# Order of high and low runs, and where the last projection is summed, in a four-layer conditional-residual kernel

## The chip, the cores and the metric

The kernel runs on one core of a Trainium2 chip. The metric is the device time of one execution in microseconds (us). The profile is that of one execution on the chip; its own time is given beside its span. Engines are named as in the profile: PE is TensorE (PEld its weight loads), DVE is VectorE, ACT is ScalarE, POOL is GpSimd, SP is SyncE, which issues most DMAs.

## The reference

Eight batches of 256 tokens with 1024 features go through four residual layers, each x = x + layer(x):

```python
# L0: dense layer plus a gated mixture of 8 rank-16 experts
base = einsum('btd,od->bto', x, W)
logits = einsum('btd,ed->bte', x, Wr); logits[..., language] += 5
gates = softmax over the two largest logits, zero elsewhere
out = base + 2 * einsum('bter,bte,eor->bto', einsum('btd,erd->bter', x, A), gates, B)
# L1: dense layer with bias, plus a per-batch matrix of signs
out = einsum('bsi,oi->bso', x, W) + b + coeff * einsum('bsi,bio->bso', x, 2 * mask - 1)
# L2: a dense layer chosen per batch by its adapter
out = einsum('bsi,boi->bso', x, weight[adapter])
# L3: a rank-16 projection chosen by the same adapter
out = einsum('bnr,bor->bno', einsum('bni,bri->bnr', x, B[adapter]), A[adapter])
```

All inputs and outputs are 32-bit floats (masks and indices are integers).

## The kernel before

**Precision in two parts.** A 32-bit operand is split into a rounded high part (type `fp32r`) and the rest, the low part. A product is high x high + high x low + low x high. `highs(n)` makes the high part of weight block n as a cast on ScalarE (tile `whi`, five buffers), `lows(n)` makes the low part as a subtraction on VectorE (tile `wlo`, four buffers).

**Stages.** Batches are taken in two groups g of four, a group in two pairs q. L0 of a group works on both pairs at once: eight products of quarter matrices (a seven-multiplication scheme with its sums), 16 slots s, with the router, the gates and the experts in between. Then each pair q passes through L1 and L2 in 16 units each. A unit is one output block m (128 of 1024 features) of one batch j of the pair: units run over m, and within m over j. The L3 work of pair q is done beside later units, by short pieces of TensorE work.

**A unit.** `two` (L526 to L542) issues eight matmuls with the high weights against 512 columns, the high and low parts of the activations side by side (L531): the high run. Then come eight matmuls with the low weights against 256 columns, the activations' high part (L540): the low run. Both sum into `po`, one half of a tile `[128, 2, 512]` of 32-bit floats in PSUM, of which there are two. The two batches of one m share a tile (a joint pair), apart from m = 7 of L1 and the last six units of all, which have one each. `early` and `mid` are lists of short pieces that run after the second high matmul and after the high run. The last unit of all uses `three` (L544): its high run takes 16 matmuls with 256 columns (L548), then the low run (L551).

**The order of the work** is written by hand. Each engine executes its instructions in the order of the program, so the slots and units are also a schedule. `unit_slot` issues for unit n, in this order: the load of a later unit (SP), stores, `evacuate` (results of the pair before leave PSUM through ScalarE and VectorE; the sum becomes the next layer's activations, split into high and low parts in the tile `hl` after L1), `highs(n + 4)`, the merging of L1's weights and masks on VectorE, `lows` of three units ahead (`LAGS` delays this near the end of L1), `fold` (a diagonal added on GpSimd), `side` (loads and preparation of L3's weights, splitting of the next pair's activations, `la_parts`, the router) and `main`, the matmuls.

**The head.** `head` issues L0's first two slots in smaller pieces. After it, `l0_slot` calls `highs(5)` and `la_parts(0, 4, 8)`, which casts half of the experts' first factor on ScalarE and subtracts on VectorE (`laghi`, `laglo`), and later `lows`. The work lists of `l0_works` are issued per slot: an entry at s before the slot's matmuls, at -s ahead of its casts. `split_gates(p0)` casts the gated expert sums (`ghi`) on ScalarE and subtracts on VectorE (`glo`); slot 5's matmuls use them. `less` in slot 4 scales two tiles by -1 on ScalarE, then GpSimd issues an accumulating DMA into each.

**The tail.** L3 of the last batch (b = 7) begins with the projection `proj`: block k of the activations against block k of the adapter's factor, with 32 columns of weights; four blocks go to four groups of 32 rows of one bank and run side by side. Blocks 0 to 3 are issued in unit 9 of the last 16. Blocks 4 to 7 are issued after the last unit (L1056), since block 7 comes out of it. A copy to SBUF (L498) and a matmul with a selection matrix (L499) sum the four groups, three times over for three row groups; `third` (L511) makes high and low parts of the result; eight matmuls (L1071) multiply by the other factor. Two blocks leave through ScalarE, after a matmul with the identity has added the old activations in PSUM (L1063); six leave through VectorE in four adds. Their stores are on the queues of SP and ScalarE. Four pieces of the batch before (`fillers`) are also left near the end: two in unit 14, two after the last unit (L1057).

Of the kernel before, what the change touches and what calls it, by code (L numbers as in the profile page):

```python
# [8 lines left out]
F32 = mybir.dt.float32  # L9
# [25 lines left out]
def kernel(ctx: ExitStack, tc: tile.TileContext, x, lang, coeff, ids,  # L35
# [449 lines left out]
    def proj(b, h, n):  # L485
        if h == 0:
            pbs[b] = bank(n, f"pb{b}")
        for g in range(4):
            mm(pbs[b][32 * g:32 * g + 32, :T], l3b[b][:, 4 * h + g, :],  # L489
               xts[b][:, 4 * h + g, :], start=(h == 0), stop=(h == 1))  # L490
        if h == 1:
            pb = pbs.pop(b)
            pr = bank(n + 2, f"pr{b}")
            prs[b] = pr
            if b == NB - 1:

                raw = gp.tile([P, T], F32, tag="lg", name="pbraw", bufs=3)
                copy(raw, pb[:, :T])  # L498
                sums[b] = lambda: mm(pr[:96, :T], sel3_raw, raw, start=True, stop=True)  # L499
                return  # L500
            hi = gp.tile([P, T], FR, tag="lg", name=f"pbhi{b}", bufs=3)
            lo = gp.tile([P, T], FR, tag="lg", name=f"pblo{b}", bufs=3)
            copy(hi, pb[:, :T])
            tt(lo, pb[:, :T], f32(hi), ALU.subtract)

            def both():
                mm(pr[:96, :T], sel3, hi, start=True, stop=False)
                mm(pr[:96, :T], sel3, lo, start=False, stop=True)
            sums[b] = both

    def third(b):  # L511
# [4 lines left out]
        tt(rt[32:64, :], pr[32:64, :T], f32(rt[32:64, :]), ALU.subtract)  # L516
        return rt

    def rank(b):
        sums.pop(b)()  # L520
        rt = third(b)
        for m in range(0, K, 2):
            fillers.append(lambda m=m: finish(b, m, rt, (0, 2)[m // 2 % 2]))


    def two(po, hi, lo, xhl, j, early=(), mid=(), late=()):  # L526


        for k in range(K):
            c = slice(k * P, (k + 1) * P)  # L530
            mm(po, hi[:, c], xhl[:, k, j].rearrange("p h t -> p (h t)"), start=(k == 0),  # L531
               stop=False)
            if k == 1:
                for f in early:
                    f()
        for f in mid:
            f()
        for k in range(K):
            c = slice(k * P, (k + 1) * P)
            mm(po[:, :T], lo[:, c], xhl[:, k, j, 0, :], start=False, stop=(k == K - 1))  # L540
        for f in late:
            f()  # L542

    def three(po, hi, lo, xhl, j):  # L544
        for k in range(K):
            c = slice(k * P, (k + 1) * P)
            for h in range(2):
                mm(po, hi[:, c], xhl[:, k, j, h, :], start=(k + h == 0), stop=False)  # L548
        for k in range(K):
            c = slice(k * P, (k + 1) * P)  # L550
            mm(po, lo[:, c], xhl[:, k, j, 0, :], start=False, stop=(k == K - 1))  # L551
# [117 lines left out]
    def l0_works(g):  # L669


        p0, p1 = pair_of(g, 0), pair_of(g, 1)
        w = {}

        def at(s, *fs):
            w.setdefault(s, []).extend(fs)

        def add(name, h, src):
            nc.gpsimd.dma_start(quad(g, name)[h], src, accum_op=ALU.add)

        def s1_add(h):
            fold_quad(quad(g, "S1")[h], h)
            add("S1", h, w0[1, 2 + h])

        def s3_add(h):
            t = quad(g, "S3")[h]
            copy(flat(t), flat(quad(g, "S2")[h]))
            fold_quad(t, h)
            add("S3", h, w0[1, 2 + h])

        def s4_add(h):
            copy(flat(quad(g, "S4")[h]), flat(quad(g, "S2")[h]))
            add("S4", h, w0[0, 2 + h])

        def less(h, name, j, i):

            t = flat(quad(g, name)[h])
            nc.scalar.mul(t, t, -1.0)  # L698
# [12 lines left out]
        if g == 0:  # L711
            at(1, constants, *both(s1_add))
            at(2, *both(less, "T1", 1, 0), lambda: router([p0]))
            at(3, lambda: weigh([p0]), lambda: expand(p0), lb_parts, *subs("S2", "A11", "S1"))
            at(4, *both(s4_add), lambda: gate(p0))
            at(5, lambda: router([p1]))
            at(6, lambda: weigh([p1]), lambda: expand(p1))
        else:
            at(0, *both(s1_add), *both(less, "T1", 1, 0))
            at(2, lambda: expand(p0))  # L720
            at(3, *subs("S2", "A11", "S1"))
            at(4, *both(s4_add), lambda: gate(p0))
# [12 lines left out]
        return w  # L735
# [59 lines left out]
    def l0_slot(n):  # L795
# [67 lines left out]

    pos_tile = {}

    def main(n):

        kind, q, m, j = slots[n]
# [6 lines left out]
        end = q == 3 and kind == "L2"  # L875
        joint = u < 10 if end else (m < K - 1 or kind == "L2")
# [54 lines left out]
    def side(n):  # L931
# [34 lines left out]
    def unit_slot(n):  # L966
# [18 lines left out]
        evacuate(bulk.pop(0) if not urgent else None)  # L985
        highs(f + HI_AHEAD)
        for work in bulk:
            work()
# [76 lines left out]
    leave = [bank(n, f"po{b}_{n}") for n in (0, 2, 1)]  # L1065

    def place(m):
        return ends[:, m % 2, :T] if m in by_act else leave[m // 2][:, m % 2 * T:m % 2 * T + T]

    for m in (0, *by_act, 1, 2, 3, 4, 5):  # L1070
        mm(place(m), at[:, m * P:(m + 1) * P], rt, start=(m not in by_act), stop=True)  # L1071

    for m0, m1, queue in ((0, 1, nc.sync), (1, 2, nc.sync), (2, 4, nc.sync), (4, 6, nc.scalar)):
        if m0 == 4:
            for i, m in enumerate(by_act):
                copy(xt[:, m, :], ends[:, i, :T])
            nc.scalar.dma_start(out[b, :, K - 2:K, :], xt[:, K - 2:K, :])
        xs = xt[:, m0:m1, :].rearrange("p m t -> p (m t)")
        tt(xs, leave[m0 // 2][:, m0 % 2 * T:m0 % 2 * T + T * (m1 - m0)], xs, ALU.add)
        queue.dma_start(out[b, :, m0:m1, :], xt[:, m0:m1, :])  # L1080


# [55 lines left out]
```

## Time and profile before

| | us |
|---|---|
| median of 3 runs | 605.03 |
| lowest, highest | 604.06, 605.21 |
| the profiled execution | 603.36 |
| its span | 601.0 |
| PE busy in the span | 593.1 |
| DVE busy | 474.2 |
| ACT busy | 385.7 |
| POOL busy | 135.2 |

The span runs from the first to the last instruction on the core; 2.3 us of the execution lie around it. The starts of matmuls are recorded and their ends are modelled, and matmuls overlap with the next one's weight load, so the distance from start to start says how long a matmul holds TensorE, not the duration in a row. A row of a group of instructions has the line of the program, the engine, the operation, output and inputs by the program's names, and a count. In a bracket at its end stands the idle time of the engine ahead of it, and what ended that. Many VectorE operations carry line 68, that of a helper, and are told apart by their tiles.

### The profile page before, as it was taken

What the parts mean: (1) busy time and instruction counts of PE and PEld (TensorE: products, weight loads), DVE (VectorE), ACT (ScalarE), POOL (GpSimd) and SP (SyncE); (2) the same over time, 40 slices, a digit from 0 to 9 for tenths busy, and PEclk for the clock granted to TensorE, in tenths of its full rate; (3) what the DMA queues carried; (4) which work ended last, traced back from release to release, by engine and by line L of the source; (5) the groups of instructions that cost most, each with busy time, mean ns of one, the idle gap of its engine ahead of it and who ended that gap; (6) DMA issues with size and microseconds to landing.
All of it is one profiled execution on the core that took longest, in us unless ns stands there. A gap on an engine that the chain in (4) does not pass through costs nothing.

```text
span 601.0 us, 8936 instructions
## 1 busy us (share of the span) xinstructions
PE 593.1 (99%) x3240; PEld 499.1 (83%) x3240; DVE 474.2 (79%) x561; ACT 385.7 (64%) x457; POOL 135.2 (23%) x174
## 2 busy tenths in 40 slices
PE   9999999999999999999999999999999999999995
PEld 7777888888888888888778888888888888888884
DVE  5579688899699899586755796789978999977853
ACT  5667566687669787543553874568866788864431
POOL 0322250114241213122110234111423111521000
PEclk9999999999999999999999999999999999999998
DMA  8987894667685877599940799836767686847504
GB/s 283 343 199 165 191 233 137 200 235 267 208 278 188 283 257 265 209 347 322 268 70 24 156 249 233 250 105 210 285 204 255 205 294 228 301 154 232 190 1 140
DMA packets 39533, 130.22 MB, mean 217 GB/s; under 512 B 4802, under 2 KB 6466, under 8 KB 38722
## 3 DMA queue, kind: packets, MB, share of 16 engines
q1 hardware_dynamic: 34594, 112.36, 53.7%
q0 software_dynamic: 4608, 16.78, 15.3%
q8 instruction: 25, 0.41, 0.3%
q10 hardware_dynamic: 288, 0.52, 0.3%
q14 instruction: 18, 0.15, 0.1%
HBM read 121.25 MB, written 8.39 MB: 216 GB/s over the span
## 4 chain that ended last, share of the span: by engine, by line
PE 97%; ACT 1%; DVE 1%; issue 0%; DVEq 0%; POOL 0%; POOLq 0%; ACTq 0%
PE po L531 39%; PE mm L599 30%; PE po L540 20%; PE pl L308 1%; PE pf L470 1%; PE pb L442 1%; PE ph L626 1%; PE ph L627 1%; PE ph L625 1%; PE warm L1010 1%; PE pb L489 0%; ACT x L698 0%; DVE c L68 0%; PE po L548 0%; PE pg L392 0%
## 5 line engine op out<-in xcount | busy, mean ns | idle before, releaser
L531 PE MATMUL po<-hl,whi 128*128 128x512 f32 x1016 | 254.5, 392 | 0.0
L531 PEld LDWEIGHTS po<-hl,whi 128*128 128x128 f32 x1016 | 182.8, 189 | 32.7
L68 DVE TENSOR_TENSOR wlo<-raw,whi 128x1024 fp32r<-128x1024 f32 x128 | 160.8, 1266 | 1.3 <-issue 1.2
L540 PEld LDWEIGHTS po<-hl,wlo 128*128 128x128 f32 x1016 | 137.6, 190 | 11.3 <-issue 1.6
L288 ACT CAST whi<-raw 128x1024 fp32r<-128x1024 f32 x128 | 133.7, 1048 | 18.0 <-PE mm L599 8.4
L540 PE MATMUL po<-hl,wlo 128*128 128x256 f32 x1016 | 142.4, 283 | 0.0
L599 PE MATMUL mm<-whi,whi 128*128 128x512 f32 x224 | 88.6, 396 | 0.0
L599 PE MATMUL mm<-wlo,whi 128*128 128x512 f32 x224 | 87.9, 392 | 0.0
L235 POOL TENSOR_TENSOR raw<-raw,ident 128x128 f32<-128x128 f32 x72 | 60.5, 843 | 115.6 <-DMA raw<-in_w 100.8
L257 ACT ACTIVATE raw<-raw,negc,c 128x1024 f32<-128x1024 int32 x64 | 79.5, 1242 | 3.9 <-DMA raw<-in_mask 3.9
L599 PE MATMUL mm<-whi,wlo 128*128 128x512 f32 x224 | 70.8, 391 | 0.0
L68 DVE TENSOR_TENSOR raw<-raw,w 128x1024 f32<-128x1024 f32 x56 | 68.8, 1228 | 1.4 <-issue 1.4
L235 POOL TENSOR_TENSOR w<-w,ident 128x128 f32<-128x128 f32 x28 | 31.1, 1112 | 167.7 <-DMA w<-in_w 120.1
L68 DVE TENSOR_TENSOR wlo<-x,whi 128x1024 fp32r<-128x1024 f32 (+1 forms) x38 | 44.8, 1187 | 11.6 <-issue 6.8
L599 PEld LDWEIGHTS mm<-whi,whi 128*128 128x128 f32 x224 | 42.2, 189 | 11.1 <-issue 1.1
L288 ACT CAST whi<-A 128x1024 fp32r<-128x1024 f32 x26 | 27.3, 1051 | 36.2 <-PE mm L599 24.5
L599 PEld LDWEIGHTS mm<-whi,wlo 128*128 128x128 f32 x224 | 42.2, 188 | 9.2 <-DVE wlo L68 0.2
L599 PEld LDWEIGHTS mm<-wlo,whi 128*128 128x128 f32 x224 | 42.2, 188 | 8.6
L572 ACT COPY c<-po 128x512 f32<-128x512 f32 (+1 forms) x34 | 18.7, 551 | 45.9 <-PE po L540 45.9
L575 ACT ACTIVATE sum<-po,b_sb 128x512 f32<-128x512 f32 (+1 forms) x36 | 23.1, 640 | 31.0 <-PE po L540 30.9
L288 ACT CAST whi<-x 128x1024 fp32r<-128x1024 f32 x34 | 35.2, 1048 | 11.1 <-PE mm L599 8.8
L68 DVE TENSOR_TENSOR c<-mm,c 128x1024 f32<-128x1024 f32 x20 | 24.4, 1221 | 21.8 <-PE mm L599 21.8
(126 smaller groups left out, 523.8 us busy)
## 6 DMA issues: line engine op xcount, KB each, us to landing
raw<-in_mask SPq DMA_DIRECT2D x64, 512.0 KB, 5.4
raw<-in_w SPq DMA_DIRECT2D x64, 512.0 KB, 4.8
w<-in_w SPq DMA_DIRECT2D x28, 512.0 KB, 3.4
out<-c SPq DMA_DIRECT2D x29, 256.0 KB, 3.2
A<-in_w SPq DMA_DIRECT2D x14, 512.0 KB, 8.6
x<-in_x SPq DMA_DIRECT2D x6, 1024.0 KB, 7.8
A<-in_w POOLq DMA_DIRECT2D x12, 512.0 KB, 8.5
x<-in_x POOLq DMA_DIRECT2D x12, 512.0 KB, 8.5
```

Source lines behind the costliest of these rows:

```text
L68: nc.vector.tensor_tensor(o, a, b, op)
L235: (eng or nc.gpsimd).tensor_tensor(t, t, ident, ALU.add)
L257: nc.scalar.activation(f32(raws[n]), raws[n], AF.Identity, bias=negc[:, b:b + 1], scale=c2[:, b:b + 1])
L288: copy(prep_hi(i), flat(source(i)))
L308: mm(pl[c:c + 32, :], wrs[:, k, :], X[g][:, j, k, :], start=(k < 4), stop=(k >= 4))
L442: mm(pb[c:c + 32, j * T:(j + 1) * T], l3b[b][:, k, :], xts[b][:, k, :], start=(k < 4), stop=(k >= 4))
L470: mm(po[:, i * T:(i + 1) * T], at[:, (m + i) * P:(m + i + 1) * P], rt, start=True, stop=True)
L531: mm(po, hi[:, c], xhl[:, k, j].rearrange("p h t -> p (h t)"), start=(k == 0), stop=False)
L540: mm(po[:, :T], lo[:, c], xhl[:, k, j, 0, :], start=False, stop=(k == K - 1))
L572: copy(xs, po[:, :, T:])
L575: nc.scalar.activation(xs, po[:, :, T:], AF.Identity, bias=b1c)
L599: mm(*args, skip_group_check=True, **kw)
```

## The change

`two` becomes `high_run` and `low_run`. The low run of a unit is put into a list, and the list is emptied at the end of a unit that closes its tile: a joint pair is issued as high run of the first batch, high run of the second, low run of the first, low run of the second. In the second unit of a joint pair `lows` is issued after `main`. In L0 of the first group, `lows(5)` is issued right after `highs(5)`, and `split_gates(p0)` moves from the start of slot 5 into slot 4, ahead of `less`. The second `la_parts` moves by two units, from 12 and 13 to 14 and 15.

At the end, blocks 4 to 6 of the last projection and one filler are issued between the high and the low run of the last unit, and their copy to SBUF follows. After the last unit the sum of the seven blocks (L499's matmul) no longer closes its group; one filler follows; then block 7 is multiplied with `b3_last`, its factor laid out three times side by side (96 columns), into the same group. `last_block` makes `b3_last` earlier on VectorE. The results of blocks 0 and 1 get places in PSUM of their own, and the order of the eight matmuls and of the leaving blocks changes.

```diff
@@ def proj(b, h, n)
-        for g in range(4):
-            mm(pbs[b][32 * g:32 * g + 32, :T], l3b[b][:, 4 * h + g, :],
-               xts[b][:, 4 * h + g, :], start=(h == 0), stop=(h == 1))
+        last = b == NB - 1
+        for k in range(4 * h, 4 * h + 4):
+            if last and k == K - 1:
+                continue
+            g = k % 4
+            mm(pbs[b][32 * g:32 * g + 32, :T], l3b[b][:, k, :], xts[b][:, k, :],
+               start=(h == 0), stop=(h == 1 or last and k == 3))
...
-                sums[b] = lambda: mm(pr[:96, :T], sel3_raw, raw, start=True, stop=True)
+                sums[b] = lambda: mm(pr[:96, :T], sel3_raw, raw, start=True, stop=False)
...
+    b3_last = wrs[:, :3, :]
+
+    def last_block():
+        nc.vector.tensor_copy(b3_last, l3b[NB - 1][:, K - 1:, :].to_broadcast([P, 3, 32]))
...
-    def two(po, hi, lo, xhl, j, early=(), mid=(), late=()):
+    def high_run(po, hi, xhl, j, early=(), mid=()):
...
+    def low_run(po, lo, xhl, j, late=()):
...
-    def three(po, hi, lo, xhl, j):
+    def three(po, hi, lo, xhl, j, mid):
...
+        for f in mid:
+            f()
@@ def l0_works(g)
-        at(-5, lambda: split_gates(p0, gts[p0]))
+        at(-5 if g else 4, lambda: split_gates(p0, gts[p0]))
@@ def l0_slot(n)
         if (g, s) == (0, 1):
             highs(5)
+            lows(5)
             la_parts(0, 4, 8)
@@ def main(n)
-            three(po, hi, lo, xh, j)
+            three(po, hi, lo, xh, j, mid=[lambda: proj(NB - 1, 1, 1), fill])
         else:
-            two(po, hi, lo, xh, j, early=early, mid=mid, late=late)
+            high_run(po, hi, xh, j, early=early, mid=mid)
+            low_runs.append(lambda: low_run(po, lo, xh, j, late=late))
         if joint and u % 2 == 0:
             return
+        while low_runs:
+            low_runs.pop(0)()
@@ def side(n)
+        if q == 3 and u == p[1] + 1:
+            last_block()
...
-            if u in (12, 13):
-                la_parts(1, 4 * (u - 12), 4 * (u - 12) + 4)
+            if u in (14, 15):
+                la_parts(1, 4 * (u - 14), 4 * (u - 14) + 4)
@@ def unit_slot(n)
-        bulk.append(lambda: lows(f + LO_AHEAD + 1 - lag))
+        low = lambda: lows(f + LO_AHEAD + 1 - lag)
+
+        behind = i % 2 and is_joint(kind, q, m, i % 16)
+        if not behind:
+            bulk.append(low)
...
         main(n)
+        if behind:
+            low()
@@ the tail
-    proj(b, 1, 1)
-    fill(2)
+    sums.pop(b)()
+    fill()
     store()
-    sums.pop(b)()
-    ends = ps.tile([P, 2, N], F32, tag="mm", name="ends")
+    mm(prs[b][:96, :T], b3_last.rearrange("p a b -> p (a b)"), xt[:, K - 1, :], start=False,
+       stop=True)
+    ends = [ps.tile([P, 2, N], F32, tag="mm", name=f"ends{i}") for i in range(2)]
     by_act = (K - 2, K - 1)
-    for i, m in enumerate(by_act):
-        mm(ends[:, i, :T], ident, xt[:, m, :], start=True, stop=False)
+    place = {m: ends[0][:, i, :T] for i, m in enumerate(by_act)}
+    for m in by_act:
+        mm(place[m], ident, xt[:, m, :], start=True, stop=False)
+    leave = [bank(n, f"po{b}_{n}") for n in (0, 1, 2)]
+    half = lambda t, i: t[:, i * T:(i + 1) * T]
+    place.update({0: half(leave[0], 0), 1: ends[1][:, 0, :T], 2: half(leave[1], 0),
+                  3: half(leave[1], 1), 4: half(leave[2], 0), 5: half(leave[2], 1)})
     rt = third(b)
...
-    for m in (0, *by_act, 1, 2, 3, 4, 5):
-        mm(place(m), at[:, m * P:(m + 1) * P], rt, start=(m not in by_act), stop=True)
+    for m in (0, 1, *by_act, 2, 3, 4, 5):
+        mm(place[m], at[:, m * P:(m + 1) * P], rt, start=(m not in by_act), stop=True)
...
+    take(0, 1, place[0], nc.sync)
+    take(1, 2, place[1], nc.sync)
+    for m in by_act:
+        copy(xt[:, m, :], place[m])
+    nc.scalar.dma_start(out[b, :, K - 2:K, :], xt[:, K - 2:K, :])
+    take(2, 4, leave[1], nc.sync)
+    take(4, 6, leave[2], nc.scalar)
```

More of the change, by code (lines that the diff above doesn't have):

```diff
@@ L494, in proj @@
             prs[b] = pr
-            if b == NB - 1:
+            if last:
                 raw = gp.tile([P, T], F32, tag="lg", name="pbraw", bufs=3)
                 copy(raw, pb[:, :T])
-                sums[b] = lambda: mm(pr[:96, :T], sel3_raw, raw, start=True, stop=True)
+                sums[b] = lambda: mm(pr[:96, :T], sel3_raw, raw, start=True, stop=False)
                 return
@@ L523, in rank @@
             fillers.append(lambda m=m: finish(b, m, rt, (0, 2)[m // 2 % 2]))
-    def two(po, hi, lo, xhl, j, early=(), mid=(), late=()):
+    def high_run(po, hi, xhl, j, early=(), mid=()):
         for k in range(K):
             c = slice(k * P, (k + 1) * P)
-            mm(po, hi[:, c], xhl[:, k, j].rearrange("p h t -> p (h t)"), start=(k == 0),
-               stop=False)
+            link(po, hi[:, c], xhl[:, k, j].rearrange("p h t -> p (h t)"), start=(k == 0),
+                 stop=False)
             if k == 1:
@@ L537, in two @@
             f()
+    def low_run(po, lo, xhl, j, late=()):
         for k in range(K):
             c = slice(k * P, (k + 1) * P)
-            mm(po[:, :T], lo[:, c], xhl[:, k, j, 0, :], start=False, stop=(k == K - 1))
+            link(po[:, :T], lo[:, c], xhl[:, k, j, 0, :], start=False, stop=(k == K - 1))
         for f in late:
             f()
-    def three(po, hi, lo, xhl, j):
+    def three(po, hi, lo, xhl, j, mid):
         for k in range(K):
@@ L864, with is_joint @@
     pos_tile = {}
+    low_runs = []
+    def is_joint(kind, q, m, u):
+        return u < 10 if (q == 3 and kind == "L2") else (m < K - 1 or kind == "L2")
     def main(n):
@@ L873, in main @@
         last = n == len(slots) - 1
-        end = q == 3 and kind == "L2"
-        joint = u < 10 if end else (m < K - 1 or kind == "L2")
+        joint = is_joint(kind, q, m, u)
         h = u % 2 if joint else 0
@@ L984, in unit_slot @@
             l0_evacuate(q // 2, 16) if q % 2 == 0 else None
-        evacuate(bulk.pop(0) if not urgent else None)
+        evacuate(bulk.pop(0) if bulk and not urgent else None)
         highs(f + HI_AHEAD)
@@ L1055, with take @@
     at, xt = l3[b], xts[b]
-    proj(b, 1, 1)
-    fill(2)
+    sums.pop(b)()
+    fill()
     store()
-    sums.pop(b)()
-    ends = ps.tile([P, 2, N], F32, tag="mm", name="ends")
+    mm(prs[b][:96, :T], b3_last.rearrange("p a b -> p (a b)"), xt[:, K - 1, :], start=False,
+       stop=True)
+    ends = [ps.tile([P, 2, N], F32, tag="mm", name=f"ends{i}") for i in range(2)]
     by_act = (K - 2, K - 1)
-    for i, m in enumerate(by_act):
-        mm(ends[:, i, :T], ident, xt[:, m, :], start=True, stop=False)
-    rt = third(b)
-    leave = [bank(n, f"po{b}_{n}") for n in (0, 2, 1)]
-    def place(m):
-        return ends[:, m % 2, :T] if m in by_act else leave[m // 2][:, m % 2 * T:m % 2 * T + T]
-    for m in (0, *by_act, 1, 2, 3, 4, 5):
[L1071 to L1077, printed above, removed]
+    place = {m: ends[0][:, i, :T] for i, m in enumerate(by_act)}
[5 more added lines that the diff above has]
+                  3: half(leave[1], 1), 4: half(leave[2], 0), 5: half(leave[2], 1)})
+    rt = third(b)
+    for m in (0, 1, *by_act, 2, 3, 4, 5):
+        mm(place[m], at[:, m * P:(m + 1) * P], rt, start=(m not in by_act), stop=True)
+    def take(m0, m1, out_of, queue):
         xs = xt[:, m0:m1, :].rearrange("p m t -> p (m t)")
-        tt(xs, leave[m0 // 2][:, m0 % 2 * T:m0 % 2 * T + T * (m1 - m0)], xs, ALU.add)
+        tt(xs, out_of, xs, ALU.add)
         queue.dma_start(out[b, :, m0:m1, :], xt[:, m0:m1, :])
+    take(0, 1, place[0], nc.sync)
[5 more added lines that the diff above has]
+    take(4, 6, leave[2], nc.scalar)
 def kernel(x, itok_B_0_7, condB_coeff, itok_B_3_7, mask_Bx4096x4096_ik1, L0_cond_W,
```

## The prediction

> **What bounds the kernel now.** I read the busy shares first, then the shares of the chain that ended last, the chain in order of time, and the waits of TensorE.
>
> ```profile
> PE 593.1 (99%) x3240; PEld 499.1 (83%) x3240; DVE 474.2 (79%) x561; ACT 385.7 (64%) x457; POOL 135.2 (23%) x174
> ...
> PE 97%; ACT 1%; DVE 1%; issue 0%; DVEq 0%; POOL 0%; POOLq 0%; ACTq 0%
> ```
>
> TensorE is busy for the whole span and carries the chain. A gain must shorten its stream, a stall in it, or the tail. Next, pieces of the chain (start, length, what):
>
> ```profile
> 24.60 5.44 PE mm L599 x24
> ...
> 115.20 1.84 PE po L531 x8
> ...
> 207.38 1.84 PE po L531 x8
> 209.22 0.95 PE po L540 x8
> 210.17 1.84 PE po L531 x8
> ...
> 587.64 1.92 PE po L548 x16
> ```
>
> From 115.20 to 207.38 lie 33 units without a break: 2.793 us each. A long run of 512-column matmuls takes 5.44/24 = 0.2267 each, a long run of 256-column ones 1.92/16 = 0.120. Eight of each should take 2.773. So a unit loses 0.020 where runs change: the eight wide ones take 1.84 instead of 1.813, the narrow ones slightly less than 0.960.
>
> TensorE's weight loads wait seldom (us, times, longest). Within the first 60 us these three touch the change:
>
> ```profile
> PEld ph L626 <- DVE wlo L68: 0.6, 1, 0.6
> PEld mm L599 <- ACT ghi L401: 0.5, 1, 0.5
> PEld mm L599 <- DVE glo L68: 0.4, 1, 0.4
> ```
>
> The timeline gives their places (start, length, engine, line, in brackets the idle time before):
>
> ```profile
> 20.71 0.98 DVE L68 TENSOR_TENSOR laglo<-c,laghi 128x512 fp32r<-128x512 f32 x1 [6.03 <-ACT laghi L651]
> ...
> 21.61 1.51 DVE L68 TENSOR_TENSOR wlo<-x,whi 128x1024 fp32r<-128x1024 f32 x1
> ...
> 23.18 0.50 PE L626 MATMUL ph<-wlo,laghi 128*128 128x512 f32 x1 [0.28 <-DVE wlo L68]
> ...
> 42.78 2.00 ACT L698 ACTIVATE x<-x 128x1024 f32<-128x1024 f32 x2
> ...
> 44.69 0.60 ACT L401 CAST ghi<-gt 128x512 fp32r<-128x512 f32 x1
> ...
> 45.34 0.72 PE L599 MATMUL mm<-ghi,lb 128*128 128x512 f32 x2
> ```
>
> VectorE idled 6.03 us, then made the low parts late; ScalarE made `ghi` after two scalings of 1 us each. The tail:
>
> ```profile
> 590.45 1.15 PE L489 MATMUL pb<-c,b 128*32 128x256 f32 x8
> 590.56 0.37 ACT L569 COPY c<-po 128x256 f32<-128x256 f32 x1 [2.50 <-PE po L551]
> ...
> 591.64 0.37 ACT L498 COPY pbraw<-pb 128x256 f32<-128x256 f32 x1 [0.71 <-PE pb L489]
> ...
> 592.77 0.37 ACT L515 CAST rt<-pr 96x256 fp32r<-96x256 f32 x1 [0.76 <-PE pr L499]
> ...
> 593.39 0.42 DVE L68 TENSOR_TENSOR rt<-pr,rt 32x256 fp32r<-32x256 f32 x1
> ...
> 594.64 1.95 DVE L68 TENSOR_TENSOR c<-po,c 128x256 f32<-128x256 f32 x4 [0.83 <-PE po L1071]
> ```
>
> **What the Trainium skill says.** "TensorE: Matmul & The Clock Gate", Step-by-step: weight loads are pulled ahead of running matmuls, and matmuls keep their order. The trace agrees: loads are busy 499.1 us beneath 593.1. The same page, Back-to-back issue gap, gives N/2.4 + 2.5 ns, 216 and 109; the trace has 227 and 120, which I use. "PSUM — Partial Sum Buffer", The four PSUM rules: two sums open in one bank and quadrant cannot both start with the clearing flag. A unit's half is 512 columns, a bank to itself, so two open sums are lawful; no run shows it yet. "SBUF — State Buffer", Who interferes with whom: a VectorE operation with two SBUF inputs contends with GpSimd reads. The 1.51 above, against about 1.22 elsewhere, agrees.
>
> **The change part by part.**
>
> *A, pairs.* H L H L becomes H H L L. Joint pairs: 7 x 4 in L1, 8 x 3 + 5 in L2, 57. In five (u = 6, 8, 14 of q = 1; 6, 8 of q = 3) other matmuls stand between the two high runs, and nothing is won. 52 x 0.020 = **-1.04**. Unseen: how long the recovery after a 16-long low run is. From 0 (the slow steps belong to the place in a run) to twice; I take once, as the low step has settled at 0.120 by its third matmul. The even low run comes 1.84 later, so its `wlo` buffer is freed later, and the subtract for unit e+4 goes behind the odd unit's matmuls, its `side` and fillers. VectorE may wait in it; behind it stands the evacuation of this pair, which can start only 0.6 after the pair's end. The subtract (1.22) begins when L(e) ends, 0.95 before the pair's end, and is done at +0.3. Cost 0. The part itself is used nearly two pairs later. No transfer is moved: loads stay at the slot's head.
>
> *B, head.* `lows(5)` goes ahead of `la_parts(0, 4, 8)`. The first of its two subtracts now falls into the 6.03 us of idleness. The second waits for its cast (done 20.16) and ends near 21.6; `laglo` (0.7 to 1.0) ends by 22.6, wanted at 22.9. The stalled matmul comes at 22.65, not 23.18 (0.53), and the next step, 0.34 here, is 0.23 again: **-0.64**. If `laglo` slips 0.3, 0.3 is left.
>
> *C, gates of the first pair.* The cast `ghi` moves ahead of the scalings: it starts at 42.8 in their place, ends near 43.4, `glo` 0.7 later, and TensorE asks at 44.5 or later. Four steps from 44.88 to 46.41 take 1.53 instead of 0.91: **-0.62**. What becomes late are the scalings and GpSimd's two accumulating DMAs for T3 behind them, by 0.6; T3 is used some 35 us on. The casts that follow on ScalarE keep their time. `la_parts(1)` moves to u = 14, 15: its two 0.69 subtracts now lie just ahead of the router, and the evacuation that `proj_pair(1)` needs stays near 303.7 while TensorE's need (304.3, last blocks at 305.2) comes a little earlier. 0; uncovered, up to 0.7.
>
> *D, tail.* Three quads of the projection and one filler go before the last low run. By start times here: 0.09 on entry, 0.24 for both passes, 0.31 to the next matmul and 0.10 on the one after (590.24 to 590.45, 591.22 to 591.53 to 591.75), and two filler matmuls 0.24: +0.98. The last narrow matmul starts at 591.22, ends 591.50. ScalarE's copy of block 7 runs 591.54 to 591.91. Meanwhile the seven blocks' sum (two passes, 0.47) and the filler (0.24) keep TensorE to 592.1; then the new 96-column matmul, priced as L499 (0.67 from start to the cast): cast 592.77 to 593.14, subtract to 593.59, first output matmul 593.64 (was 593.86). Its sum now has a bank that only it writes, so the first add starts 0.43 after it, not 0.78: 594.07 against 594.64. Four adds (1.95), the last issue and its landing as before: **-0.57**, from -1.0 to +0.3 because the switch to four-byte matmuls and the filler's cost are unproven. `last_block` copies 96 columns on VectorE, below the 0.42 of the 512-column copy, in a stage where VectorE has 16.4 of 27.4 us: 0.
>
> Sum: -1.04 - 0.64 - 0.62 - 0.57 = **-2.87**. The profiled run took 603.36 (span 601.0, 2.3 around it), so 600.5 there; its median is 605.03, which gives **602.2**.
>
> **The rivals.**
> *Seam stall, slower.* The first L2 pair's odd high run starts 0.95 earlier, 158.78 for 159.73, while the last `hl` part is written 159.18 to 159.87. The trace puts the semaphore wait on the load of the eighth matmul, 161.12, thus 160.17, so there is 0.3 of margin. If the wait falls on the first matmul instead, the run stalls 1.1 at each of four seams: 4.5 - 2.9 = +1.6, **606.7**. It decides from about 1.0 a seam.
> *No recovery to save:* A gives 0, **603.2**. For it: I infer the cause. Against: a high run broken by other matmuls (u = 14, q = 3) is slow in its later steps too.
> *Early time swallowed:* TensorE comes 1.26 earlier through the rest of L0 and meets VectorE chains or DMA sums that don't move; B and C give 0, **603.4**. Against: those chains start from `glo` and from buffers that TensorE frees.
> *Tail even:* **602.7**. *A, B and C all fail:* 604.5, no change that can be measured.
>
> **How the numbers follow.** Main case 0.56; tail even 0.10; no recovery 0.10; swallowed 0.10; all fail 0.06; seam 0.08. A measurement here tells about 0.2%, 1.2 us. Faster 0.86, of which I give 0.02 to "same" for cases that add up: 0.84; same 0.08; slower 0.08. Low end: A twice, 601.2. High end 604.2: two of the failures together; outside it lie the seam and most of "all fail".
>
> **What would show it.** A: the period of a pair 5.566 instead of 5.587, with one slow start per pair. B, C: the three waits above gone, no new one in L0. D: the last projection's matmuls before L551's run, the first add 1.9 to 2.2 us before the last DMA issue, and within 0.5 of the first output matmul. Wrong if the chain shows VectorE `hl` or `wlo` before a high or low run, or if the tail's new matmul starts much later than 0.1 after block 7's copy.

## Result, and the profile after

| us | before | after |
|---|---|---|
| median of 6 runs each | 603.66 | 601.22 |
| lowest, highest | 602.99, 605.21 | 600.67, 601.64 |
| the profiled execution | 603.36 | 601.06 |
| its span | 601.0 | 598.9 |

The ratio of after to before is 0.996, with a 95% interval of 0.9946 to 0.9973. The difference of the medians is 2.44, that of the profiled executions 2.30; the forecast was 2.87. The forecast of 602.2 stood on the median of the first three runs of before, 605.03; with three further runs the median of all six is 603.66. That base is 1.4 lower, the gain 0.4 smaller, and so the measured time is 1.0 below the forecast.

The page of the changed kernel, the lines that answer to those shown of before:

```profile
PE 591.4 (99%) x3240; PEld 500.2 (84%) x3240; DVE 474.5 (79%) x562; ACT 385.5 (64%) x457; POOL 129.5 (22%) x174
...
PE 97%; ACT 1%; issue 0%; DVE 0%; DVEq 0%; POOL 0%; POOLq 0%; ACTq 0%
```

TensorE is still busy for the whole span and carries the chain. It has the same 3240 matmuls and is busy for 1.7 us less. Since the ends of matmuls are modelled, that figure doesn't tell faster steps from shorter waits; the table of places below does. Next, waits of TensorE's weight loads, from the first 60 us and from the seam between the two groups (us, times, longest):

```profile
PEld mm L614 <- ACT c L759: 0.5, 1, 0.5
...
PEld pb L442 <- DVE wlo L68: 0.4, 1, 0.4
```

The three waits that the prediction named are gone, and these two were not there before. Their places, with those of the steps B and C, in the timeline of the changed kernel (start, length, engine, line):

```profile
20.01 1.23 DVE L68 TENSOR_TENSOR wlo<-A,whi 128x1024 fp32r<-128x1024 f32 x1 [4.53 <-DMA A<-in_w]
21.15 0.95 DVE L68 TENSOR_TENSOR laglo<-c,laghi 128x512 fp32r<-128x512 f32 x1
...
22.56 0.40 PE L641 MATMUL ph<-wlo,laghi 128*128 128x512 f32 x1
...
42.12 0.61 ACT L401 CAST ghi<-gt 128x512 fp32r<-128x512 f32 x1
...
44.41 0.63 PE L614 MATMUL mm<-ghi,lb 128*128 128x512 f32 x2
...
45.48 1.05 ACT L288 CAST whi<-x 128x1024 fp32r<-128x1024 f32 x1
46.44 1.99 ACT L759 COPY c<-mm 128x1024 f32<-128x1024 f32 x2
...
46.98 0.39 PE L614 MATMUL mm<-glo,lb 128*128 128x512 f32 x1
47.48 0.50 PE L614 MATMUL mm<-whi,whi 128*128 128x512 f32 x1
...
301.49 1.22 DVE L68 TENSOR_TENSOR wlo<-x,whi 128x1024 fp32r<-128x1024 f32 x1
302.63 0.68 DVE L68 TENSOR_TENSOR c<-po,c 128x512 f32<-128x512 f32 x1
```

The experts' matmul comes at 22.56 (23.18 before), the gated one at 44.41 (45.34 before). But the matmul that follows the one at 46.98 needs a bank of PSUM that ScalarE has yet to copy out. The copy (L759) stands behind a weight cast and starts at 46.44; half of it is done near 47.45, and TensorE goes on at 47.48, 0.50 after the matmul ahead of it, where 0.23 is usual. At 301.49 VectorE makes the low part that the change put behind unit 15, and only then evacuates (302.63) what TensorE needs. The same places in the timeline of the kernel before: the copy behind its cast, the matmul that needs the bank, and the evacuation, which the projection needed from 304.3 on:

```profile
46.15 1.05 ACT L288 CAST whi<-x 128x1024 fp32r<-128x1024 f32 x1
47.30 1.01 ACT L744 COPY c<-mm 128x1024 f32<-128x1024 f32 x1
...
48.50 0.39 PE L599 MATMUL mm<-whi,whi 128*128 128x512 f32 x1
...
303.70 0.68 DVE L68 TENSOR_TENSOR c<-po,c 128x512 f32<-128x512 f32 x1
```

Last, for the changed kernel again, the pairs in the units and the tail:

```profile
116.80 3.82 PE L614 MATMUL po<-hl,whi 128*128 128x512 f32 x16
120.45 2.08 PE L614 MATMUL po<-hl,wlo 128*128 128x256 f32 x16
122.36 3.82 PE L614 MATMUL po<-hl,whi 128*128 128x512 f32 x16
...
590.21 0.62 PE L1090 MATMUL pr<-c,wrs 128*96 128x256 f32 x2
...
590.87 0.37 ACT L519 CAST rt<-pr 96x256 fp32r<-96x256 f32 x1 [0.76 <-PE pr L1090]
591.27 0.42 DVE L68 TENSOR_TENSOR rt<-pr,rt 32x256 fp32r<-32x256 f32 x1 [0.17 <-ACT rt L519]
...
592.17 0.42 DVE L68 TENSOR_TENSOR c<-po,c 128x256 f32<-128x256 f32 x1 [0.48 <-PE po L1103]
...
594.15 0.34 ACTq L1109 DMA_DIRECT2D out<-c  x1
```

To put the 2.1 us of span in their places, I take the start of each matmul in one trace less that of its counterpart in the other. How this difference changes from place to place is the time won or lost there:

| place | won (-) or lost (+), us | forecast |
|---|---|---|
| first 12 us, ahead of any change | -0.17 | none |
| B, slot 1 of L0, at 23 us | -0.55 | -0.64 |
| C, slot 5, at 45 us | -0.59 | -0.62 |
| slot 6, at 47 us: the copy out of PSUM | +0.38 | none |
| rest of L0 of the first group | -0.08 | none |
| A, all units (batch pairs 0 and 1: 0.51; 2 and 3: 0.47) | -0.98 | -1.04 |
| seam between the groups, at 303 us | +0.17 | 0 |
| D, to the issue of the last store | -0.65 | -0.57 |
| landing of the last store, 3.6 for 3.3 | +0.31 | 0 |

They add up to -2.16, which is the difference of the spans (601.03 and 598.87 before rounding). The forecast sum was 2.87, 0.71 too large: 0.86 by the copy at 47 us, the seam and the landing, which were not in it, and 0.18 by A, B and C, less 0.08 that D won more and 0.25 that nobody forecast.

### The profile page after: what moved, and what is told of

Same layout as the page of the kernel before. It is cut to its first block, busy times and chain, and to the rows that moved or that the text cites. A ratio compares the mean times of both kernels' runs of the same rounds, so it can differ in the third digit from the quotient of the medians.

```text
span 598.9 us, 8938 instructions
## 1 busy us (share of the span) xinstructions
PE 591.4 (99%) x3240; PEld 500.2 (84%) x3240; DVE 474.5 (79%) x562; ACT 385.5 (64%) x457; POOL 129.5 (22%) x174
## 4 chain that ended last, share of the span: by engine, by line
PE 97%; ACT 1%; issue 0%; DVE 0%; DVEq 0%; POOL 0%; POOLq 0%; ACTq 0%
PE po L614 59%; PE mm L614 29%; PE pl L308 1%; PE pf L470 1%; PE pb L442 1%; PE ph L640 1%; PE ph L641 1%; PE ph L642 1%; PE warm L1041 1%; ACT whi L288 1%; PE pb L493 0%; ACT x L713 0%; PE po L561 0%; PE pg L392 0%; PE pt L319 0%
## 5 line engine op out<-in xcount | busy, mean ns | idle before, releaser
L614 PE MATMUL po<-hl,whi 128*128 128x512 f32 x1016 | 244.8, 391 | 0.0
L614 PEld LDWEIGHTS po<-hl,whi 128*128 128x128 f32 x1016 | 186.0, 188 | 35.6
L614 PEld LDWEIGHTS po<-hl,wlo 128*128 128x128 f32 x1016 | 130.4, 191 | 7.2 <-issue 2.5
L614 PE MATMUL po<-hl,wlo 128*128 128x256 f32 x1016 | 133.4, 283 | 0.0
L235 POOL TENSOR_TENSOR raw<-raw,ident 128x128 f32<-128x128 f32 x72 | 55.4, 771 | 129.2 <-DMA raw<-in_w 110.7
L235 POOL TENSOR_TENSOR w<-w,ident 128x128 f32<-128x128 f32 x28 | 29.6, 1059 | 164.9 <-DMA w<-in_w 131.6
```

The costliest lines, as they stand in the source:

```text
L235: (eng or nc.gpsimd).tensor_tensor(t, t, ident, ALU.add)
L614: mm(*args, skip_group_check=True, **kw)
```

## The experiments

Each edit is made on the changed kernel unless the text says otherwise. Two profiled executions of one and the same kernel differ: e10_changed, the changed kernel again, had a span of 599.3, almost 0.5 longer than the trace above; of this 0.14 arose in the first 10 us, where TensorE still waits for data, and 0.28 at the copy at 47 us. So the verdicts rest on where a trace gains and loses, with spans and medians beside them. The medians of before on the same chips lay between 603.28 and 603.52. "The start" below means these first microseconds, "the seam" the passage between the two groups near 303 us, and "the evacuation" the addition on VectorE there that takes results out of PSUM.

### Pairs taken apart (e1_no_pairs)

```diff
-        if joint and u % 2 == 0:
-            return
         while low_runs:
             low_runs.pop(0)()
+        if joint and u % 2 == 0:
+            return
...
-        behind = i % 2 and is_joint(kind, q, m, i % 16)
+        behind = False
```

> The changed kernel with each unit's low run put back behind its own high run, and the low parts made ahead of the matmuls again; head, gates and tail stay changed. Theory of the change of runs (a high run after a low run loses 0.020 us in all, one after a high run nothing): 49 pairs lose 0.020 each, +0.97, and the 0.17 that slot 0 of the second group's L0 lost to the low part behind unit 15 comes back: span 598.9 + 0.80 = 599.7, median about 602.0 where the changed kernel has 601.2; every ordinary pair 5.586 from start to start, not 5.566. Rival, the slow steps belong to the first places of a unit's sum, whatever stands before: no pair changes, span 598.7.

Measured: span 599.6, median 602.45, ratio to before 0.9984 (0.9977 to 0.999). Against the changed kernel every ordinary pair loses 0.020, with no exception, and the pairs at which the change had won nothing lose nothing: in all 0.98. The rival, which adds nothing, falls. Two other terms differ: the start was 0.28 earlier by chance (with 0.05 at the copy at 47 us, 0.33), and at the seam 0.14 was lost where I had expected 0.17 back: with the low part ahead of the router's steps these begin later, and the evacuation (302.93) with them. That the sum came out near 599.7 is partly luck. VectorE has one low part too many ahead of that evacuation, wherever it stands; the seam is taken up below.

### Twice as many changes of runs (e6_four_runs)

```diff
-    def high_run(po, hi, xhl, j, early=(), mid=()):
+    def high_run(po, hi, xhl, j, early=(), mid=(), lo=None):
...
+            if k == 3 and lo is not None:
+                for i in range(4):
+                    link(po[:, :T], lo[:, i * P:(i + 1) * P], xhl[:, i, j, 0, :], start=False,
+                         stop=False)
...
     def low_run(po, lo, xhl, j, late=()):
-        for k in range(K):
+        for k in range(4, K):
...
-            high_run(po, hi, xh, j, early=early, mid=mid)
+            high_run(po, hi, xh, j, early=early, mid=mid, lo=lo)
```

on top of e1_no_pairs.

> As e1_no_pairs, but each unit is cut into high 4, low 4, high 4, low 4, so that it has two changes from low to high instead of one; same matmuls, same sums. Theory of the change of runs: 63 more changes, each 24 (the first four steps of a high run, 7, 9, 2 and 6 ns above 226.6) less 7 or 8 (the first two of a low run, below 120): +1.0, up to +1.26 if the whole 0.020 comes again: span 600.6 to 600.9 where e1_no_pairs has 599.6. Rival, place in the unit's sum: the second four high matmuls follow the pattern of places 5 to 8, and nothing is added: 599.6. Second rival, what counts is how long the low run was: after four narrow matmuls the loss is half, +0.5, 600.1.

Measured: span 601.5, median 603.94. In the units 1.6 us were added to e1_no_pairs. My count in the expectation was wrong: the 63 should be about 127 units, each with one change more, so the sizes given there come to twice as much: 2.1 to 2.5 for the first theory, 1.0 for the second rival. The 1.6 lies between them; 1.6/127 is 0.0126 for each. Mean steps from start to start tell why, in ns:

| | high run | low run |
|---|---|---|
| 8 high, 8 low (before) | 233.7 235.7 228.4 232.3 231.0 226.6 226.7 226.5 | 113.5 119.1 120.1 119.8 120.2 120.0 120.0 119.8 |
| 16 high, 16 low (after) | 233.3 235.8 228.3 232.5 230.8 226.6 226.7 226.7, then eight of 226.6 to 226.7 | 113.4 119.2, then fourteen of 120.0 |
| 4 high, 4 low | 234.1 234.5 232.0 228.4 | 117.4 119.5 118.7 118.4 |

The row of four is the mean of both high runs of a unit, which agree within 0.2 ns. The second four high matmuls of a unit step like the first four, not like places 5 to 8: the slow steps belong to the change, not to the place in the sum. After sixteen narrow matmuls the recovery is the same as after eight: 20.3 ns in all against 20.2. After four it is 16.3, less than the full loss of the first theory and more than the half of the second rival. Per extra change that is 2 x 16.3 - 20.2 = 12.4 ns, which answers to the 12.6.

### The head without the early low part (e2_no_head)

```diff
             highs(5)
-            lows(5)
             la_parts(0, 4, 8)
```

> The changed kernel without the early low part in L0's slot 1. My theory: the experts' matmul near 23 us waits for its low part again, +0.56, and since ScalarE's queue at slots 4 to 6 follows TensorE's matmuls, the later stall at 47 us stays as it is: span 599.5. Rival, the stall at 47 us is set by work that doesn't depend on TensorE, and takes up what the head loses: +0.18, span 599.1, with the stall at 47 us shrunk from 0.38 to nothing.

Measured: span 599.8, median 601.73. Neither number holds. At 23 us only 0.22 was lost, with TensorE 0.48 early from the start, at 47 us 0.75 more than in the changed kernel, and 0.35 more at the seam at 303 us. The cause stands in ScalarE's timeline of e2_no_head:

```profile
39.75 1.05 ACT L288 CAST whi<-x 128x1024 fp32r<-128x1024 f32 x1 [0.68 <-DMA x<-in_x]
...
46.91 1.91 ACT L759 COPY c<-mm 128x1024 f32<-128x1024 f32 x2
```

A weight cast of slot 4 waited 0.68 for a transfer of x. Everything behind it in the queue came late, the copy at the end by 0.47 (46.91 for 46.44), while TensorE came 0.26 earlier than in the changed kernel: together about the 0.75. At the seam too a load was late, that of an L3 factor for which ScalarE waits: it landed at 290.4, not 288.9, and the evacuation came at 303.53, not 302.63. The stall at 47 us, then, is set by a transfer as well as by ScalarE's order, and in the traces that have it, it ran from 0.33 to 1.13. Nor has step B one price. The late subtract took 1.51 in the trace of before, 1.49 here and in e12_pairs_seam, and 2.21 in e9_pairs_alone, each time beside additions of GpSimd, where 1.23 is usual, and the stall was longest where the subtract was. In before the subtract ahead of it was slowed as well (`laglo`, 0.98; here 0.69), which is about the difference between the 0.55 that step B won and the 0.22 lost here.

### The gates late again (e3_late_gates)

```diff
-        at(-5 if g else 4, lambda: split_gates(p0, gts[p0]))
+        at(-5, lambda: split_gates(p0, gts[p0]))
```

> The changed kernel with the gates of the first pair split at the start of slot 5 again, as before. My theory: the wait at 45 us is back, +0.57, and the copy out of PSUM that held TensorE at 47.0 to 47.5 us is in time again, -0.38, since TensorE comes later and ScalarE doesn't: +0.19, span 599.1. Rival, the two stalls are independent of each other: +0.57, span 599.5.

Measured: at 45 us 0.58 lost, at 47 us 0.38 won, 0.2 together, as my theory had it; the two stalls are one queue, and the rival falls. The span was 599.6 all the same, since 0.36 of it had arisen in the first 10 us and another 0.16 came in small pieces later. The median was 601.6. With the copy where it is, then, step C is worth 0.2.

### The old tail (e4_old_tail)

```diff
-            three(po, hi, lo, xh, j, mid=[lambda: proj(NB - 1, 1, 1), fill])
+            three(po, hi, lo, xh, j, mid=[])
...
-    sums.pop(b)()
-    fill()
+    proj(b, 1, 1)
+    fill(2)
     store()
+    sums.pop(b)()
```

with the tail of before after it.

> The changed kernel with the tail of before: the last four blocks projected after the last unit, two fillers there, the old order of output blocks. My theory: the last DMA is issued 0.57 later than in the changed kernel, and its landing takes 3.3 us in place of 3.6, since the stores lie further apart: span +0.31, 599.2. As the prediction had it (the same landing): +0.57, 599.5. Rival, tail even: 598.9.

Measured: span 599.3, median 601.52. The last store is issued at 594.94, 0.79 later than in the changed kernel, 0.14 of which had arisen before the tail: 0.65, the same as between before and after. The landing, 3.28 for 3.61, gave 0.33 of it back. This is the view of the store's line for e4_old_tail (its last figure is the longest, that of the last store):

```profile
DMA to landing us min/median/max: 1.9/3.2/3.3
```

### One store less (e7_one_store_less)

```diff
     for m in by_act:
         copy(xt[:, m, :], place[m])
-    nc.scalar.dma_start(out[b, :, K - 2:K, :], xt[:, K - 2:K, :])
     take(2, 4, leave[1], nc.sync)
```

> The changed kernel without the store of output blocks 6 and 7 of the last batch, which is left out (256 KB). Queue theory of the landing (the last store took 3.63 from its issue to its landing because the transfers of the stores before it were still under way): one store less frees the engines, the last store lands 0.3 to 0.7 sooner, span 598.2 to 598.6. Fixed-latency theory: the last store takes 3.6 again, span 598.9, less 0.03 for the issue that is left out ahead of it on ScalarE.

The same view of the changed kernel and then of this one:

```profile
DMA to landing us min/median/max: 1.9/3.5/3.6
```

```profile
DMA to landing us min/median/max: 1.9/2.1/2.8
```

The last store lands 0.8 sooner after its issue, a little more than the queue theory gave, and the span is 598.3 although TensorE was 0.17 later. The fixed latency falls. The five stores of the last batch are a megabyte. From the first issue to the last it is 1.53 in both kernels, and SyncE's other two keep their places between; only the store of blocks 6 and 7, the one left out here, is nearer to the last: 0.96 ahead of it, where it was 1.42 in before. SyncE's last store, on another queue, also took 3.53 for 3.23, so more than the order within one queue is at work; that the stores share the DMA engines fits, but was not tried apart from this. With the bytes moved nearer to the end the last store takes longer: that is the 0.3 by which the tail's 0.65 shrank.

### Two moves against the new stalls (e5_two_moves; e11_two_moves_beside is the same kernel, beside e10_changed)

```diff
-        highs(f + HI_AHEAD)
+        highs(f + HI_AHEAD - ((g, s) == (0, 5)))
...
-        if behind:
+        if behind and (q, i % 16) != (1, 15):
             low()
```

> The changed kernel with two moves against the two new stalls: in slot 5 of the first group the cast of one weight block waits until after ScalarE's copy out of PSUM, and the low part behind unit 15 of pair 1 is made in the next slot instead, after the evacuation. My theory: the stalls at 47 us (0.38) and at 303 us (0.17) are ScalarE's and VectorE's order alone: both gone, -0.55, span 598.35, median about 600.7. Rival, the moved cast and low part are late in turn, and a new wait of the same size stands one slot later: 0, span 598.9.

> The changed kernel itself, so that the next run has it on the same chip: 601.2, ratio to the kernel before 0.996, span 598.9 give or take the 0.3 that the first 10 us vary.

> The kernel of e5_two_moves beside the changed kernel on one chip. If its two moves are worth what the trace gave them (0.38 and 0.12), its median is 0.5 below that of e10_changed, 600.7, and its ratio to the kernel before 0.995; if the start's variation swallows them, the medians are equal within 0.2.

Measured: e5_two_moves 600.66 (ratio 0.995), with a span of 599.0, since the start had been late by 0.64; e10_changed 601.56, span 599.3; e11_two_moves_beside 600.64, ratio 0.995 (0.9937 to 0.9964), span 598.1. On the chip that had both, the highest of six times with the two moves (600.98) is below the lowest of six of the changed kernel (601.03). In the trace both waits are gone: 0.40 won at 47 us and 0.12 at 303 us against the first trace of the changed kernel. The timeline of e11_two_moves_beside:

```profile
45.81 1.01 ACT L759 COPY c<-mm 128x1024 f32<-128x1024 f32 x1 [0.41 <-PE mm L614]
...
300.88 0.68 DVE L68 TENSOR_TENSOR c<-po,c 128x512 f32<-128x512 f32 x1
301.48 1.21 DVE L68 TENSOR_TENSOR wlo<-x,whi 128x1024 fp32r<-128x1024 f32 x1
```

ScalarE now waits for TensorE ahead of the copy (0.41), not the other way round, and the evacuation precedes the low part. No wait took their places, so the rival falls. This version beats both kernels, by 0.5% the one before.

### The experts' subtracts early again (e8_parts_early)

```diff
-            if u in (14, 15):
-                la_parts(1, 4 * (u - 14), 4 * (u - 14) + 4)
+            if u in (12, 13):
+                la_parts(1, 4 * (u - 12), 4 * (u - 12) + 4)
```

> The changed kernel with the second half of the experts' factor split in units 12 and 13 again, as before, the low part behind unit 15 staying where it is. My theory: the two subtracts (0.69 each) leave the stretch ahead of the router, the router begins about 1 us sooner, and the evacuation at 302.6 us is ready before TensorE asks: the stall at 303 us is gone, -0.17, span 598.7. Rival, the router waits for TensorE's transposes and only the low part behind unit 15 delays the evacuation: the stall stays, 598.9. Third, the subtracts at units 12 and 13 delay an evacuation there instead: 599.0 or more.

Measured: span 600.6, median 602.2, and 1.7 lost against the changed kernel: 1.36 at the router's transposes at 294 us and 0.33 at the seam at 303 us. The third case came nearest, at another place and far dearer; my theory fell. The two subtracts are not what delays. The timeline of e8_parts_early:

```profile
292.62 0.62 ACT L666 CAST laghi<-c 128x512 fp32r<-128x512 f32 x1 [2.67 <-DMA c<-in_la]
...
294.61 1.06 ACT L312 COPY lg<-pl 128x512 f32<-128x512 f32 x2
...
295.24 1.14 PE L319 MATMUL pt<-ident,lg 128*128 128x128 f32 x8 [1.08 <-ACT lg L312]
```

Ahead of them ScalarE casts a factor whose load had only landed near 292.6, and the copies of the router's logits, which TensorE asks for at 294.0 in the changed kernel, stand behind that cast.

### The pairs alone (e9_pairs_alone), and with the seam put in order (e12_pairs_seam)

Both are the kernel before with the pairs, and with its own head, gates and tail. e9_pairs_alone has the subtracts in units 12 and 13; e12_pairs_seam adds two edits:

```diff
-            if u in (12, 13):
-                la_parts(1, 4 * (u - 12), 4 * (u - 12) + 4)
+            if u in (14, 15):
+                la_parts(1, 4 * (u - 14), 4 * (u - 14) + 4)
...
-        if behind:
+        if behind and (q, i % 16) != (1, 15):
             low()
```

> The kernel before with the pairs alone (with the low part of a pair's second unit made behind it): head, gates, tail and the place of the experts' subtracts in units 12 and 13 as before. Theory of earlier time against a fixed load: the stall that stood at the router in e8_parts_early came from the factor's load, which lands near 292 to 292.6 us whatever TensorE does, while TensorE came 1.5 us sooner than before; with the pairs alone it comes only 0.5 sooner and had 0.8 in hand, so the stall is 0 to 0.25, and the whole is -0.97 plus at most 0.45: span 600.0 to 600.5, median 0.5 to 1.0 below the kernel before. Rival, the order of the pairs itself puts the subtracts in the way: the stall of 1.2 stands here too, span 601.2 or more, no gain.

> The kernel of e9_pairs_alone with two edits at the seam between the groups: the experts' subtracts in units 14 and 15, and the low part behind unit 15 of pair 1 made after the next slot's evacuation. My theory: the 0.74 that e9_pairs_alone lost between 293 and 305 us was ScalarE waiting for a load ahead of the router's copies (0.26) and VectorE making a low part ahead of the evacuation (0.48); both are out of the way, so TensorE keeps all of the pairs' 0.97 from the first unit to the tail, and the ratio to the kernel before is about 0.998. Rival, TensorE comes earlier than something at the seam that these two don't move: 0.3 or more is lost there again.

Measured: e9_pairs_alone 603.58, ratio 0.9995 (0.9983 to 1.0006): no gain that a measurement can tell. Against before the pairs won their 0.98 and the way to the second group took 0.74: 0.26 at the router, at the upper end of what I had given it, and 0.48 at the evacuation, more than I had. The head lost another 0.56, mostly at the late low part of step B. So the span of 601.4 is the number of my rival, but its stall of 1.2 at the router did not come. The timeline of e9_pairs_alone shows both causes:

```profile
293.08 0.62 ACT L666 CAST laghi<-c 128x512 fp32r<-128x512 f32 x1 [2.06 <-DMA c<-in_la]
...
295.07 1.06 ACT L312 COPY lg<-pl 128x512 f32<-128x512 f32 x2
...
303.67 1.22 DVE L68 TENSOR_TENSOR wlo<-x,whi 128x1024 fp32r<-128x1024 f32 x1
304.81 0.68 DVE L68 TENSOR_TENSOR c<-po,c 128x512 f32<-128x512 f32 x1
```

ScalarE stands 2.06 for a load that lands at 293.1, and the logits follow two microseconds later. The load is not fixed near 292 to 292.6, as I had written: it was issued 0.90 later than in before and landed 1.03 later, about half of it with the late head, and in the traces of other variants it landed between 290.2 and 292.7. So part of the 0.26 is the load's own lateness in this execution, and how large a part one trace doesn't tell. VectorE makes the low part of unit 15 behind the router's steps instead of ahead of them, as before had it, and the evacuation starts at 304.81 instead of 303.70.

e12_pairs_seam: 601.94, ratio 0.9972 (0.996 to 0.9984), span 599.9. TensorE loses 0.04 on the way to the second group instead of 0.74, and keeps 0.94 of the pairs' 0.98; another 0.23 of its span came with the head. These two kernels show both causes together. In the changed kernel e8_parts_early moves the subtracts by themselves, and e11_two_moves_beside the low part, with a move at 47 us that lies elsewhere in the trace.

## Why the prediction was right, and where not

**A, right, term by term nearly.** It took 0.020 for each of 52 pairs. The trace shows 0.020 for each of 50 and 0.014 lost at two: 0.98 for 1.04. Those two are the two pairs that it counted too many, units 4 and 5 of batch pairs 1 and 3. Their short pieces stand behind both high runs and not between them, so the rule of the prediction didn't exclude them; why they lose, the runs don't show. "Once" was the right choice between nothing and twice: the recovery after sixteen narrow matmuls is that after eight. The subtract that the prediction moved behind the odd unit held nothing up inside the units, as said; at unit 15 of pair 1 it did, for there the router's work stands between.

**B, right in place, the size not a constant.** The main trace gave 0.55 for 0.64, and `laglo` ran its 0.95 beside GpSimd, as the upper of the two lengths assumed. But what the step saves is a stall whose length follows GpSimd's additions beside it. The Trainium skill's page "SBUF — State Buffer", Who interferes with whom, says that a VectorE operation with two SBUF inputs contends with a GpSimd operation that reads SBUF; 1.49 to 2.21 for a subtract that takes 1.23 alone agrees. It goes both ways: in the changed kernel, where the subtract at 20.01 kept its 1.23, the addition of GpSimd that began meanwhile took 1.26, against 0.46 for two in the trace of before that had begun ahead of VectorE's. Step B itself varies too: in e4_old_tail, which has it, `laglo` took 1.49 for 0.95, and 0.24 was lost there.

**C, the cost of the step mis-sized.** The four steps shrank by 0.59 for 0.62, and what was named as becoming late (scalings, accumulating DMAs) did no harm. "The casts that follow on ScalarE keep their time" was true and was the trouble: the last of them came 0.67 sooner (45.48 for 46.15), no more than TensorE had already won before step C, and TensorE came another 0.59 earlier to the copy behind it. That gave 0.38 back. This is the rival of early time swallowed, in one slot rather than throughout, and the prediction's own sign, no new wait in L0, did not hold. It could have been read in the trace of before, shown above, a dozen matmuls further on: there ScalarE's copy (47.30, 1.01) was ready only some 0.2 ahead of TensorE's need at 48.50. In the trace after, the copy starts 0.86 sooner and the need comes 1.29 sooner, at 47.21.

**`la_parts` and the seam at 303 us, the step that failed.** It was set at 0, with up to 0.7 if uncovered, on the ground that the evacuation stays near 303.7 while TensorE's need comes a little earlier. The need came 1.5 earlier (all that had been won by then), the evacuation 1.07, and 0.17 was lost. And the move was taken for a side effect, while it carries the rest. With the subtracts left where they were, the earliness of TensorE meets a load. With the seam that costs 1.7 in the changed kernel, and 0.74 for the pairs alone, three quarters of what they win.

**D, right to the last issue, wrong at the landing.** The insertion, the copy, the 96-column matmul and the first add came within 0.1 of the times given, once the 1.82 won ahead of them is taken off, and the last issue 0.65 sooner for 0.57. "The last issue and its landing as before" is the clause that failed: the landing took 3.6 for 3.3, with the store of blocks 6 and 7 now nearer to the last one.

**The slower rival** did not come: no high run waits at the seams from L1 to L2. The measured 601.22 lies 1.0 below the main case of 602.2 and inside the range from 601.2 to 604.2 by 0.02, which is luck: the base of three runs was 1.4 too high and the forecast gain 0.4 too large, and the two errors worked against each other.

## What to carry to other kernels

When an engine that bounds a kernel gains time, look at the next things that it asks for which do not come earlier with it: a load with a landing time of its own, a copy queued behind other work. Here the pairs' 0.98 was worth 0.2 until two pieces of work elsewhere were moved, and nearly all of it afterwards. Price the cover of each such wait against all the time won ahead of it, not against that of its own step. At the end of a kernel, look at the bytes that are still to leave: here an issue of the last store 0.65 earlier won only 0.34, since a store ahead of it had come nearer.

## What the runs showed of the hardware

- A run of 512-column matmuls after a run of 256-column ones steps at 234, 236, 228, 232 and 231 ns before it settles at 226.6; the first two narrow ones after it are 6.5 and 0.9 shorter than 120.0. The net loss of 20 ns is the same after 8 and after 16 narrow matmuls and 16 after 4. What causes it, the runs don't tell. The Trainium skill's page "TensorE: Matmul & The Clock Gate", Back-to-back issue gap, has N/2.4 + 2.5 ns for the gap of a single matmul taken by itself, which comes to an estimate of 216 and 109; the settled steps of these long runs, 226.6 and 120.0, lie above both.
- A subtract on VectorE of 128x1024 values, mostly 1.20 to 1.23, took up to 2.21 beside GpSimd's additions in the head, and an addition there 0.46 to 1.83.
- The last of five stores (256 KB of 1 MB) took 3.6 from issue to landing, 3.3 with one earlier store of 256 KB issued 0.46 further ahead of it, and 2.8 with that store left out.
- The changed kernel's runs lie within 1.1 us, those of the kernel before within 2.2 to 2.9. The late low part of step B is not enough to explain it: e9_pairs_alone, which has it, lies within 2.8 (14 runs), but e12_pairs_seam, which has it too and differs from e9_pairs_alone at the seam alone, within 1.05 (7 runs). The cause stays open.
